# Building a 0/1 matrix from eight columns, moving one batch's sums, and interleaving two projections of v with the first scores

## The chip, the cores and the metric

The kernel runs on one core of a Trainium2 chip. The metric is the device time in microseconds (us). A core has five engines that run side by side and meet at semaphores: PE (TensorE, matrix products; PEld are its weight loads), DVE (VectorE), ACT (ScalarE), POOL (GpSimd) and SP (SyncE, which here only issues DMAs). Each engine works through its own instructions in order. ACT and POOL can issue DMAs too.

## The reference

The reference is two transformer-like layers over x of 4 batches with 512 tokens of 128 values. Only the first layer is touched by the change:

```python
xn = _layernorm(x)
s = _L0_attn_ref(xn, Wq, Wk, Wv, Wo, betas, memory0, z0)
g = _silu(_L0_ffn_ref(xn, Wr, Wg, Wu, Wd, Sg, Su, Sd, expert_bias))
x = x + s * g
```

`_L0_ffn_ref` is a mixture of 8 experts of width 64 with a shared expert: the logits `xn @ Wr` choose two experts for each token, whose probabilities stand in a row `rw` of 8 values (the others are 0); the result is `sum_e rw[e] * (silu(xn @ Wg[e]) * (xn @ Wu[e])) @ Wd[e]` plus the shared expert. `_L0_attn_ref` has 16 heads of width 64 and goes through the sequence in segments of 64 tokens:

```python
scores = q @ k.T * scale            # masked inside the segment
att_dot = softmax(scores) @ v
att_mem = sq @ M / (sq @ Z.T)       # sq = elu(q) + 1, state of all earlier segments
M, Z = M + sk.T @ v, Z + sk.sum()   # sk = elu(k) + 1
out = (gate * att_mem + (1 - gate) * att_dot) @ Wo
```

## The kernel before

The tokens stand as 16 tiles of 128, four to a batch. The program is written out as straight code. Most instructions are pinned (`self.pin`, `mm1`, `act1`, `vec1`): each engine keeps them in the order in which the program names them. Plain GpSimd instructions and DMAs are not pinned, and are placed by a scheduler.

**Loads.** `load_first` issues the 16 tiles of x (12 from SP, 4 from ACT), then from POOL wr, ebias, sg, su and sd, and from SP, behind x, wg, wu, wd and the weights of the attention (lines 120 to 168).

**The first feed-forward stage**, `norm_ffn0`. PE is first warmed with 16 products. `begin0` builds on POOL what the routing needs: `pick0`, a matrix of 96 x 512 zeros and ones in bf16 that spreads the 8 weights of a token over the 64 rows of each expert (line 356 on: a memset, six `affine_select`, each over 32 rows, and a copy to bf16), a bf16 identity, and two zeroed tiles `parts0`. Then batch 0 is brought in: `sums` (line 307: two VectorE instructions, bn_stats and bn_aggr, for each tile), `norm_scale` (root on ACT, reciprocal on DVE), `normed` (line 325: four VectorE instructions that write xn), `turned` (four transposes on PE, one copy to xnT on ACT), `logits`, `shared` (products pg_s and pu_s with sg and su), `chosen` and `weights` (VectorE: the two largest logits of each token, their probabilities in three bf16 parts).

The main loop has 16 steps (b, j), batch by pair of experts. A step makes pg and pu on PE (with wg and wu), h = silu(pg) on ACT, then the preceding step's `down` (products eo with wd, of h that is done by then), pw = pick0 x part on PE, and on DVE h = h * pu (line 559) and h = h * pw (line 560). At the end of a step stands a list `then[(b, j)]` of what prepares later batches. In the kernel before, `sums` of batch 3 stands in the list of step (0, 2), behind `shared_h` and `weights` of batch 1; the list of step (0, 3) has the root over batches 2 and 3 and the normalization of batch 2.

**The first attention**, `attn0`. A half batch h (256 tokens, four segments, each for two independent row groups) is projected by the 12 chunks that `project(h)` returns: 4 of k and 4 of q (`chunk`: products pp, evicted by ACT to pj), 4 of v (`chunk_v`: product pv, evicted to a tile vt, by DVE for h of 0 and 1 and by ACT later, then stored by a DMA from SP to vd in DRAM). `values(n)` loads v of segment n back from vd in another order, as vone (two DMAs from SP). PSUM is shared by `narrow` tiles (two buffers: pp, pv, pk, pa) and `wide` tiles (three buffers: sc, mm, mu, dot, po). vt has two buffers.

The work of a segment n is: `elu_exp` (two ACT instructions) and `elu` (one DVE instruction) for q (0) and k (1); `scores` (products sc, DVE minimum to E); `scores_exp` (ACT); `memory` (products mm, DVE reciprocal and t, POOL times gate); `keys` (transposes pk, ACT copy sk); `update` (products mu, DVE sum to mz); `attend` (products dot, DVE to t, POOL times gate2 and plus t); `attended` (transposes pa). Before the loop over the 32 segments a prologue projects half batch 0, and starts segment 0 and half of segment 1. In the loop, iteration n does the scores of n + 1, memory, update and attend of n, and some chunks of the next half batch's projection: four in iterations 0, 1 and 2, where iteration 0 takes the chunks of v of half batch 1, and 1 and 2 those of k and q.

After these stages follow the second layer's mixture of experts and its attention. They are not changed.

Of the kernel before, what the change touches and what calls it, by code (L numbers as in the profile page):

```python
# [12 lines left out]
F32 = mybir.dt.float32  # L13
# [26 lines left out]
NE, F0 = 8, 64  # L40
# [62 lines left out]
def bc(ap, axis, n):  # L103

    shape = list(ap.shape)
    return ap.unsqueeze(axis).to_broadcast(shape[:axis] + [n] + shape[axis:])


class Kernel:
# [242 lines left out]
    def begin0(self, pool):  # L352


        nc = self.nc
        pick = pool.tile([96, NE // 2, 2, F0], F32, name="pick0")
        nc.gpsimd.memset(pick, 1.0)
        for at in range(0, 96, 32):
            for sign in (1, -1):
                part = pick[at : at + 32]  # L360
                nc.gpsimd.affine_select(
                    out=part, in_=part, pattern=[[-2 * sign, NE // 2], [-sign, 2], [0, F0]],
                    compare_op=ALU.is_ge, fill=0.0, base=0, channel_multiplier=sign,
                )
        self.pick0 = pool.tile([96, NE // 2, 2, F0], BF16, name="pick0b")
        nc.gpsimd.tensor_copy(self.pick0, pick)
        self.identb = pool.tile([P, P], BF16, name="identb")
        nc.gpsimd.tensor_copy(self.identb, self.ident)
        self.parts0 = []
        for k in range(2):  # L370
            t = pool.tile([P, 4, 96], BF16, name=f"parts{k}")
            nc.gpsimd.memset(t, 0.0)
            self.parts0.append(t)

    def norm_ffn0(self, layer, aside=None):
# [4 lines left out]
        nc, tc = self.nc, self.tc  # L380
        v = nc.vector
        xnT, g0 = ([self.of_batch(w, layer, b) for b in range(B)] for w in ("xnT", "g"))
        with tc.tile_pool(name=f"f0_{layer}", bufs=1) as pool, tc.tile_pool(
            name=f"f0p_{layer}", bufs=1, space=PSUM
# [17 lines left out]
            now, xn, lg, rw, part, hs, eo = {}, {}, {}, {}, {}, {}, {}  # L402
# [91 lines left out]
            def down(b, j, h, w):  # L494
# [12 lines left out]
            first = {(b, 0): [(spread, b)] for b in range(B)}  # L507
            then = {
                (0, 0): [(turned, 1), (sums, 2), (more, 1)],
                (0, 1): [(logits, 1), (shared, 1), (chosen, 1)],  # L510
                (0, 2): [(shared_h, 1), (weights, 1), (sums, 3)],
                (0, 3): [(self.norm_scale, mv, rstd, slice(8, 16)), (normed, 2)],
                (1, 0): [(turned, 2), (normed, 3)],
                (1, 1): [(logits, 2), (shared, 2), (chosen, 2)],
# [53 lines left out]
    def attn0(self, xnT, g0, stack, psum, between):  # L568
# [4 lines left out]
        nc, tc = self.nc, self.tc  # L573
# [27 lines left out]
        def project(h):  # L601


            if h >= 2 * B:
                return []
            qkv[h] = dst = [
                pool.tile([P, 32, 64], F32, name=f"pj{h}_{wi}", tag=f"pj{wi}")
                for wi in range(2)
            ]
            vd[h] = drams.tile([2, P * 16, DK], F32, name=f"vd{h}", tag="vd")  # L610
            def chunk_v(p, k):
                ps = narrow(f"pv{h}_{p}_{k}")
                self.mm1(
                    ps, lhsT=xnT[h // 2][:, h % 2 * 2 + p, :],
                    rhs=self.wqkv[2][:, k * S : (k + 1) * S], start=True, stop=True,
                )
                t = pool.tile([P, S], F32, name=f"vt{h}_{p}_{k}", tag="vt")
                if h > 1:
                    self.act1(t, ps, AF.Copy)
                else:  # L620
                    self.vec1(nc.vector.tensor_copy(t, ps))
                nc.sync.dma_start(
                    out=vd[h][p].rearrange("(q k c) d -> k q (c d)", k=2, c=8)[k], in_=t
                )

            def chunk(wi, cq):
                ps = narrow(f"pp{h}_{wi}_{cq}").rearrange("p (c k) -> p c k", c=4)
                for c4 in range(4):
                    c = cq * 4 + c4
                    for p in range(2):  # L630
                        self.mm1(
                            ps[halves[p], c4, :],
                            lhsT=self.wqkv[wi][:, c * 64 : c * 64 + 64],
                            rhs=xnT[h // 2][:, h % 2 * 2 + p, :], start=True, stop=True,
                        )
                view = dst[wi].rearrange("d k (t c) -> d (k t) c", c=16)
                self.act1(
                    view[:, :, cq * 4 : cq * 4 + 4], ps.rearrange("d c k -> d k c"), AF.Copy
                )
            qk = [(lambda wi=wi, cq=cq: chunk(wi, cq)) for wi in (1, 0) for cq in range(4)]  # L640
            v = [(lambda p=p, k=k: chunk_v(p, k)) for p in range(2) for k in range(2)]
            return v + qk if h else qk[:4] + v + qk[4:]
# [5 lines left out]
        def scores(n):  # L648

            q, k = blocks(n, 0), blocks(n, 1)  # L650
            ps = wide(f"sc{n}")
            for hp in range(4):
                for p in range(2):
                    for a in range(2):
                        self.mm1(
                            ps[halves[a], p, hp * 64 : hp * 64 + 64],
                            lhsT=k[halves[p], 2 * hp + a, :], rhs=q[halves[p], 2 * hp + a, :],
                            start=True, stop=True,
                        )
            e = pool.tile([P, 2, 4, LSEG], F32, name=f"E{n}", tag="E")  # L660
            self.vec1(nc.vector.tensor_tensor(  # L661
                e, ps[:, :, 0:256].rearrange("p x (hp c) -> p x hp c", hp=4),
                bc(bc(self.cap, 1, 4), 1, 2), ALU.min,
            ))
            seg[n]["e"] = e

        def scores_exp(n):
            e = seg[n]["e"]
            self.act1(e, e, AF.Exp, scale=1.0 / math.sqrt(DK))
# [4 lines left out]
        def elu_exp(n, w):  # L674
            t = pool.tile([P, 8, 64], F32, name=f"elu{w}{n}", tag=f"elu{w}")
            up = pool.tile([P, 8, 64], F32, name=f"up{w}{n}", tag="up")
            self.act1(t, blocks(n, w), AF.Exp)
            self.act1(up, blocks(n, w), AF.Relu)
            seg[n][w] = t, up

        def elu(n, w):

            t, up = seg[n][w]
            self.vec1(nc.vector.scalar_tensor_tensor(t, t, 1.0, up, ALU.min, ALU.add))  # L684
            seg[n][w] = t
# [11 lines left out]
        def keys(n):  # L697
            t = pool.tile([P, 4, 2, DK], F32, name=f"sk{n}", tag="sk")
            self.act1(t, turn(n, seg[n][1], "pk"), AF.Copy)
            seg[n]["sk"] = t  # L700

        def values(n):

            for p in range(2):
                src = vd[n // 4][p].rearrange("(s hp r) d -> s r hp d", s=4, hp=4)
                nc.sync.dma_start(out=vone[n % 4][:, :, p, 0:DK], in_=src[n % 4])
# [107 lines left out]
        for i, chunk in enumerate(todo):  # L814
            chunk()
            if i == 4:
                elu_exp(0, 1)
            if i == 7:
                elu(0, 1)
            if i == 9:  # L820
                keys(0)
        for n in range(2):
            values(n)
        elu_exp(0, 0)
        scores(0)
        scores_exp(0)
        elu(0, 0)
        elu_exp(1, 1)
        elu(1, 1)
        for n in range(nseg):  # L830
            if n == 0 or n % 4 == 3:
                todo = project((n + 1) // 4 + 1)
            each = 4 if n < 3 or n % 4 != 2 else 0
            nxt = n + 1 < nseg
            more = nxt and not last(n + 1)
            if n + 2 < nseg:
                values(n + 2)
            if nxt:
                elu_exp(n + 1, 0)
                scores(n + 1)  # L840
            memory(n)
            if nxt:
                elu(n + 1, 0)
            if n > 1:
                attended(n - 2)
            if more:
                keys(n + 1)
            if not last(n):
                update(n)
            for f, *args in between.get(n - 0.5, []):  # L850
                f(*args)
            attend(n)
            ahead = n + 2 < nseg and not last(n + 2)
            if ahead:
                elu_exp(n + 2, 1)
            chunks, todo = todo[:each], todo[each:]
            for chunk in chunks[:1]:
                chunk()
            if nxt:
                scores_exp(n + 1)  # L860
            if ahead:
                elu(n + 2, 1)
            for chunk in chunks[1:]:
                chunk()
            for f, *args in between.get(n - 0.25, []):
                f(*args)
            if n % 4 == 2 and n > 4:
                output(n // 4 - 1)
            if not nxt:
                attended(n - 1)  # L870
            for f, *args in between.get(n, []):
                f(*args)
# [1601 lines left out]
```

## Time and profile before

| | us |
|---|---|
| median of 3 runs (from 721.18 to 721.28) | 721.2 |
| the profiled execution | 722.03 |
| its span, first to last instruction | 720.4 |
| PE busy, of the span | 678.1 (94%) |
| DVE busy | 503.7 (70%) |
| ACT busy | 490.9 (68%) |
| POOL busy | 345.7 (48%) |
| first feed-forward stage, up to the first product of the attention | 79.0 |
| attention up to the first product of half batch 1's keys | 107.2 |
| mean granted TensorE clock | 0.991 |

The profile is that of one execution. A row of a timeline or a group reads: start, length, engine, line, operation, what it writes and reads by the names in the program, form, and in brackets the idle time of the engine before it and what ended that. Products, activations and copies that go through helpers all stand at line 336 or 339; the tile's name tells them apart. The granted clock is the share of full speed at which PE was allowed to run. A matrix product of f32 with 512 columns shows as two records.

### The profile page before, as it was taken

How to read it: one execution, taken by the hardware profiler on the slowest of the kernel's cores; microseconds unless marked ns; L12 is line 12 of the kernel's file. 1: busy time of each engine (PE TensorE's matmuls, PEld its weight loads, DVE VectorE, ACT ScalarE, POOL GpSimd, SP SyncE). 2: the span in 40 equal slices, each digit the busy share in tenths (PEclk: the TensorE clock that was granted, in tenths of full speed). 3: DMA queues.
4: the chain of work that ended last, by engine and by line, in shares of the span. 5: the costliest groups of instructions: out<-in, count | busy, mean ns of one | idle time of the engine just before them, and what ended most of it. 6: DMA issues, size and time to landing. Idle time of an engine off the chain costs nothing.

```text
span 720.4 us, 23270 instructions
## 1 busy us (share of the span) xinstructions
PE 678.1 (94%) x9888; PEld 418.1 (58%) x9891; DVE 503.7 (70%) x1078; ACT 490.9 (68%) x809; POOL 345.7 (48%) x381
## 2 busy tenths in 40 slices
PE   7999879999999899979999999999999999999994
PEld 4666557878879677867777783332335233422433
DVE  6776365667576775884549324889896999588854
ACT  3423457877777885653563468989987899899830
POOL 7680027566666574693754423411482844312250
PEclk9999999999999998999999999999999999999999
DMA  7740143231331312100034249967949494955200
GB/s 184 135 134 0 56 129 79 67 106 40 97 106 33 105 30 78 39 12 1 1 98 153 74 146 213 255 168 174 240 148 221 109 250 129 217 143 144 59 17 19
DMA packets 84847, 79.42 MB, mean 110 GB/s; under 512 B 42512, under 2 KB 73520, under 8 KB 81664
## 3 DMA queue, kind: packets, MB, share of 16 engines
q1 hardware_dynamic: 81904, 75.12, 39.6%
q0 software_dynamic: 2256, 2.47, 1.8%
q8 instruction: 80, 1.31, 0.8%
q10 hardware_dynamic: 576, 0.26, 0.1%
q14 instruction: 31, 0.25, 0.1%
HBM read 51.62 MB, written 26.21 MB: 108 GB/s over the span
## 4 chain that ended last, share of the span: by engine, by line
PE 70%; DVE 12%; ACT 10%; issue 4%; DMA 2%; POOL 1%; SPq 0%; DVEq 0%; ACTq 0%; POOLq 0%
PE acc L336 9%; PE pp L336 8%; ACT e L339 7%; PE eo L336 7%; PE po L336 5%; PE ph L336 4%; PE b L336 3%; PE pv L336 3%; PE s L336 3%; PE pl L336 3%; PE sc L336 2%; PE pa L785 2%; PE pg L336 2%; PE pu L336 2%; PE dot L336 2%
## 5 line engine op out<-in xcount | busy, mean ns | idle before, releaser
L339 ACT ACTIVATE e<-s 128x1024 f32<-128x1024 f32 x124 | 121.9, 1056 | 13.8 <-PE s L336 12.7
L336 PE MATMUL acc<-e,strip 128*32 128x512 f32 x1000 | 124.6, 598 | 0.9 <-DVE e L1874 0.9
L339 ACT ACTIVATE e<-e 128x1024 f32<-128x1024 f32 x104 | 107.4, 1094 | 0.0
L736 POOL TENSOR_TENSOR t<-t,gate 128x512 f32<-128x512 f32 x32 | 49.7, 1554 | 66.0 <-DVE t L717 66.0
L336 PEld LDWEIGHTS acc<-e,strip 128*32 128x32 f32 x1000 | 28.6, 109 | 70.4 <-issue 59.2
L774 POOL TENSOR_TENSOR t<-t,gate 128x512 f32<-128x512 f32 x32 | 50.7, 1585 | 31.0 <-DVE sums L773 24.6
L339 ACT ACTIVATE pj<-pp 128x512 f32<-128x512 f32 x64 | 38.5, 602 | 21.2 <-PE pp L336 21.0
L684 DVE SCALAR_TENSOR_TENSOR elu<-elu,up 128x512 f32<-128x512 f32 x60 | 48.0, 801 | 5.3 <-ACT up L339 5.3
L661 DVE TENSOR_TENSOR E<-sc,cap 128x512 f32<-128x512 f32 x32 | 22.0, 688 | 40.2 <-PE sc L336 40.2
L339 ACT ACTIVATE h<-ph 128x1024 f32<-128x1024 f32 x20 | 20.5, 1023 | 38.3 <-PE ph L336 31.0
L339 ACT ACTIVATE attT<-pa 128x128 f32<-128x128 f32 x128 | 25.0, 284 | 28.5 <-PE pa L785 28.1
L336 PE MATMUL s<-q,k 64*128 64x512 bf16 x256 | 40.9, 382 | 3.5 <-ACT e L339 3.3
L336 PEld LDWEIGHTS <-k 64*128 64x128 bf16 x256 | 8.8, 94 | 59.6 <-issue 58.6
L775 POOL TENSOR_TENSOR t<-t,t 128x512 f32<-128x512 f32 x32 | 41.8, 1307 | 2.5
L336 PE MATMUL eo<-w_out,h 128*128 128x128 f32 x320 | 39.6, 278 | 0.0
L336 PEld LDWEIGHTS eo<-w_out,h 128*128 128x128 f32 x320 | 37.6, 192 | 3.4 <-issue 1.9
L339 ACT ACTIVATE elu<-pj 128x512 f32<-128x512 f32 x60 | 38.5, 642 | 0.1
L1714 POOL TENSOR_TENSOR pr<-pr,pr 128x512 f32<-128x512 f32 x14 | 22.5, 1629 | 33.4 <-DVE pr L1709 33.3
L339 ACT ACTIVATE up<-pj 128x512 f32<-128x512 f32 x60 | 38.4, 639 | 0.0
L336 PE MATMUL pp<-xnT,l0Wq 128*64 128x128 f32 x512 | 31.2, 277 | 3.2 <-ACT attT L339 2.2
L1623 DVE TENSOR_TENSOR second<-second,first 128x1024 f32<-128x1024 f32 x16 | 27.0, 1694 | 9.0 <-DMA second<-qf 9.0
L1157 POOL TENSOR_SCALAR th<-th 128x512 f32<-128x512 f32 x4 | 2.5, 617 | 64.2 <-ACT th L339 64.2
(331 smaller groups left out, 1641.9 us busy)
## 6 DMA issues: line engine op xcount, KB each, us to landing
vd<-vt SPq DMA_DIRECT2D x32, 256.0 KB
vone<-vd SPq DMA_DIRECT2D x64, 128.0 KB
first<-qe SPq DMA_DIRECT2D x8, 1024.0 KB
second<-qf SPq DMA_DIRECT2D x16, 512.0 KB
third<-qf SPq DMA_DIRECT2D x32, 256.0 KB
qf<-qT SPq DMA_DIRECT2D x64, 64.0 KB
k<-kd SPq DMA_DIRECT2D x16, 256.0 KB
q<-qd SPq DMA_DIRECT2D x16, 256.0 KB
```

The costliest lines, as they stand in the source:

```text
L336: return self.pin(self.nc.tensor.matmul(*args, **kw))
L339: return self.pin(self.nc.scalar.activation(*args, **kw))
L661: self.vec1(nc.vector.tensor_tensor(e, ps[:, :, 0:256].rearrange("p x (hp c) -> p x hp c", hp=4), bc(bc(self.cap, 1, 4), 1, 2), ALU.min,))
L684: self.vec1(nc.vector.scalar_tensor_tensor(t, t, 1.0, up, ALU.min, ALU.add))
L736: nc.gpsimd.tensor_mul(t, t, self.gate)
L774: nc.gpsimd.tensor_mul(t, t, gate2)
L775: nc.gpsimd.tensor_add(t, t, seg[n]["t1"])
L785: self.pin(nc.tensor.transpose(ps[:, hp, :], seg[n]["att"][:, hp].rearrange("i p v -> i (p v)"), self.ident,))
L1157: self.pool1(self.nc.gpsimd.tensor_scalar(t, t, 0.5, 0.5, ALU.mult, ALU.add))
L1623: self.vec1(self.nc.vector.tensor_mul(t, t, self.first1[mm][:, two]))
L1714: self.nc.gpsimd.tensor_add(self.prod1[b, m], self.prod1[b, m], t)
```

## The change

```diff
@@ begin0
-        pick = pool.tile([96, NE // 2, 2, F0], F32, name="pick0")
+        pick = pool.tile([96, NE // 2, 2], F32, name="pick0")
         nc.gpsimd.memset(pick, 1.0)
...
-                    out=part, in_=part, pattern=[[-2 * sign, NE // 2], [-sign, 2], [0, F0]],
+                    out=part, in_=part, pattern=[[-2 * sign, NE // 2], [-sign, 2]],
...
-        nc.gpsimd.tensor_copy(self.pick0, pick)
+        nc.gpsimd.tensor_copy(self.pick0, bc(pick, 3, F0))
@@ norm_ffn0
-                (0, 1): [(logits, 1), (shared, 1), (chosen, 1)],
-                (0, 2): [(shared_h, 1), (weights, 1), (sums, 3)],
+                (0, 1): [(logits, 1), (shared, 1), (chosen, 1), (sums, 3)],
+                (0, 2): [(shared_h, 1), (weights, 1)],
@@ attn0
+        ahead = project(1)
         for n in range(2):
             values(n)
+        ahead.pop(0)()
         elu_exp(0, 0)
+        elu(0, 0)
         scores(0)
-        scores_exp(0)
-        elu(0, 0)
         elu_exp(1, 1)
         elu(1, 1)
+        ahead.pop(0)()
+        scores_exp(0)
         for n in range(nseg):
-            if n == 0 or n % 4 == 3:
+            if n % 4 == 3:
                 todo = project((n + 1) // 4 + 1)
-            each = 4 if n < 3 or n % 4 != 2 else 0
+            elif n == 0:
+                todo = ahead
+            each = 2 if n == 0 else 4 if n < 3 or n % 4 != 2 else 0
```

The 0/1 matrix is made as 96 x 8 values; the copy to bf16 repeats each of them 64 times (`bc` is a view with a step of 0). The sums of batch 3 are named one step sooner, behind `chosen` of batch 1, which puts them before the two multiplications of h of step (0, 2) instead of before those of step (0, 3).

In the attention, the first chunk of v of half batch 1 goes before the first scores, and the second between `scores` of segments 0 and 1; the other two remain in iteration 0. In the engines' orders this gives: PE pv, sc (segment 0), pv, sc (segment 1), mm, pk, mu, dot, pv, pv; DVE vt, elu of q of segment 0, E of segment 0, elu of k of segment 1, vt, E of segment 1. `scores_exp(0)` stands behind `elu_exp(1, 1)` on ACT. On SP, the store of the first chunk comes before the last of the loads of segment 3's v, and the second right after that load. Number and shapes of products, activations and DMAs are as before.

## The prediction

> **What bounds the kernel now.** I read the chain of waits over the first 125 us, then each engine's timeline there, then busy time by stretches. The page's summary of the chain says what kind of kernel this is: TensorE (PE) carries most of it, so a microsecond of PE idle time that ends on another engine is a microsecond of the end, unless a later wait takes it back.
>
> ```profile
> PE 70%; DVE 12%; ACT 10%; issue 4%; DMA 2%; POOL 1%; SPq 0%; DVEq 0%; ACTq 0%; POOLq 0%
> ```
>
> The change touches three places, and the chain (start, length, what) leaves PE in all of them:
>
> ```profile
> 6.15 2.88 DVE xn L325 x4
> ...
> 11.37 1.91 PE pg_s L336 x2
> ...
> 32.65 2.05 PE eo L336 x16
> ```
>
> VectorE's timeline (the bracket is the idle time before) shows the first: four normalizations take 2.87 us, and the same four take 1.11 us ten microseconds later.
>
> ```profile
> 6.15 2.87 DVE L325 TENSOR_SCALAR xn<-x,mv,rstd 128x128 f32<-128x128 f32 x4
> ...
> 16.04 1.11 DVE L325 TENSOR_SCALAR xn<-x,mv,rstd 128x128 f32<-128x128 f32 x4
> ...
> 25.47 0.69 DVE L559 TENSOR_TENSOR h<-h,pu 128x512 f32<-128x512 f32 x1 [1.45 <-PE pu L336]
> ```
>
> GpSimd's timeline shows what ran beside the slow four: the wide selects of the 0/1 matrix, each next to one normalization, one every 0.72 us on both engines. The second line is a select of few columns, 0.2 us each.
>
> ```profile
> 5.35 3.59 POOL L361 TENSOR_SCALAR_AFFINE_SELECT pick<-pick 32x512 f32<-32x512 f32 x5
> ...
> 39.08 0.59 POOL L1193 TENSOR_SCALAR_AFFINE_SELECT of<-of 128x4 f32<-128x4 f32 x3
> ```
>
> Busy time by stretch (PE, PEld, DVE, ACT, POOL, then the granted clock) shows that the thin first stretch is followed by 3.4 us at half the clock:
>
> ```profile
> 7.39:10.80 3.41, 1.69 (x10) 1.12 (x10) 3.09 (x11) 0.75 (x2) 3.06 (x7) 1.00 0.43 114
> 10.80:14.21 3.41, 3.41 (x8) 1.86 (x8) 2.63 (x20) 2.43 (x5) 3.37 (x6) 0.50 1.14 272
> 270.21:273.63 3.42, 2.56 (x12) 1.26 (x10) 0.35 (x2) 1.52 (x3) 2.67 (x2) 1.00 0.56 203
> ```
>
> And PE's timeline at the start of the attention shows holes in front of nearly every step, ended by VectorE:
>
> ```profile
> 95.05 1.00 PE L336 MATMUL mm<-mz,elu 64*64 64x65 f32 x32 [0.95 <-DVE elu L684]
> 96.97 0.63 PE L691 MATMUL pk<-ident,elu 128*128 128x128 f32 x4 [0.92 <-DVE elu L684]
> ...
> 101.24 1.12 PE L336 MATMUL pv<-l0Wv,xnT 128*128 128x512 f32 x2 [0.64 <-DVE vt L621]
> 103.05 1.12 PE L336 MATMUL pv<-l0Wv,xnT 128*128 128x512 f32 x2 [0.69 <-DVE vt L621]
> ```
>
> **Part 1, the 0/1 matrix.** GpSimd: the memset (0.54) becomes some 0.15 by the smallest memsets of its timeline; six selects of 0.67 become six of 0.2 by the row above; the copy to bf16 still writes 96x512 and keeps its 0.61. Nothing waits for the matrix itself: it was ready at 11.3 and is first read at 17.4. So by itself this is worth nothing; the 3.2 us that GpSimd gains are hidden, and its later loads merely start sooner. What counts is the normalization beside it, which is on the chain.
> How much faster does it get? A memset, the last selects and a copy still run on GpSimd from 6 to 7.7. The Trainium skill (SBUF — State Buffer, "Who interferes with whom") says that a VectorE operation in a two-port mode and a GpSimd operation exclude each other for the whole instruction. By that rule alone each of the four still waits out one short operation: 4 x (0.28 + 0.2) = 1.9, a gain of 1.0. The nearest row is the normalization at 35.56, which took 1.11 with two GpSimd copies of 128x128 inside it: a gain of 1.76. Against it stands a VectorE cast of 0.70 instead of 0.17 at 40.74, amid 42 tiny memsets. I take the row, 1.76, and keep 1.0 as the other end.
> What is late next: PE at present reaches pg_s at 11.2 and runs it, pu_s and half of pg at half clock (1.91 against 0.96 at 21.83). With 1.76 less, pg_s starts at 9.4, and the stretch 7.39 to 10.80 has more work. Counting each record's columns at 0.43 us per 512, that stretch held 11% array work and 270.21 to 273.63 held 37%; both were followed by half clock. The least that was not is 43%, at 75.7. With pg_s from 9.4 it is about 45%, so the drop should go. Then PE would reach pg at 11.0; but pg needs wg and pu needs wu, whose transfers land at 12.5 and 13.6 by the trace's landing events (packets under 512 bytes, which are these two, run until 12.9). So the loads bind: pu starts at 13.6 instead of 15.5. GpSimd's load l1bqf, now issued near 7.9 instead of 11.25, puts one packet of 4 KB and 0.16 us on each DMA engine, before or amid wg: 13.8. Gain **1.7**. The parts of the router weights (VectorE, ready at 15.4 - 1.8 = 13.6) do not bind pu, and wd lands at 17.4, ahead of its first use near 18. With the low end, 1.0, the drop stays, and pu_s and pg run at half speed: gain 1.3.
>
> **Part 2, sums of batch 3.** Four pairs of statistics, 29.53 to 31.13, are 1.60 us ahead of the two multiplications for h of step (0,3); PE waits for these until 32.65. They move to 23.9, where VectorE sits idle 1.45 us until pu (row above): they end at 25.5 and delay the multiplication at 25.47 by 0.1, and the one after it waits for pw until 26.51 anyway. The x tiles have been in since 10.6. Then h is ready at 31.0 and PE, free after the transposes of part 1's weights at 31.08, goes on without its 1.41 us hole. Next would be ScalarE: its two table loads around the root (27.98 and 31.57, 1.28 each) run one after the other once the sums are early, so the next Silu is at 30.9 instead of 32.87, and part of batch 1 near 31.4, before PE wants it at 32.9. The normalization of batch 2 begins at 31.2 instead of 32.7. Gain 32.65 - 31.08 = **1.55**.
>
> **Part 3, projections of v.** No work is added; two of the four chunks (PE 0.95, VectorE copy 0.69, one DMA from SP each) move ahead. I replay the engines in the old times, from 92.27, where PE ends pp and used to wait 0.7 for ScalarE. pv 0 runs there to 93.2, sc 0 to 93.7 (0.3 later than before), pv 1 to 94.65, sc 1 to 95.2. VectorE: copy of pv 0 to 93.95, elu(0,0) to 94.8, E 0 to 95.4, elu(1,1) to 96.0 (was 96.8, since ScalarE now makes its inputs before the exponential of E 0), copy of pv 1 to 96.6, E 1 to 97.2. PE: mm at 95.2, pk at 96.1 (was 96.97), mu 96.6, dot at 97.25 when E 1 has freed its PSUM buffer (was 98.04). The remaining two chunks follow to 99.6 without the DMA waits at 103.3 and 105.1, because only two are left for two buffers. VectorE then goes through the first segment (rm, t, elu, mz, rd, t, sums) to 100.4, one copy to 101.05, elu(2,1) to 102.25 (it took 1.29 beside GpSimd's multiplication before, and stands beside it again), the last copy to 102.9, E 2 to 103.5. PE: pk at 102.3, dot at 103.55, the pp chunks at 104.05. They were at 107.18: gain **3.1**.
> Bounds: if the copies' 2 x 0.69 ahead of elu and E are paid in full because VectorE is the bound from 93 to 103, it is 1.7; 3.6 if elu(2,1) is not held up. On SP, the store of pv 0 now stands ahead of the last of segment 3's v loads; that load is wanted after 113, so the wait costs nothing. The other loads queue behind stores that come earlier than before. On ScalarE the exponential of E 0 is behind two more activations (1.04 us), but E 0 itself is ready only at 95.4, as they end.
>
> **Sum.** 1.7 + 1.55 + 3.1 = 6.35. The profiled execution took 722.03 (span 720.4), 0.8 over the median of 721.2: its span would be 714.0, itself 715.7, and the median **714.9**. Behind 107 us the same instructions follow in the same order, all earlier, with no load from the start still pending.
>
> **Rivals.**
> - The clock moves elsewhere (0.3). The half-speed stretches begin on a grid of 3.41 us. If the grid keeps still, the thin part at 270 to 275 falls 6.35 earlier on it. Its half speed (273.6 to 280.5) costs about 2.5 us: sc to dot take 4.7 instead of some 2.6, lp 0.5 to 0.8 more. If it vanishes: 712.4. If another thin place takes a new one, such as the new hole at 100.5 to 102.3 or the stretch at 249 (about 30% on some grids), one window costs up to 1.7: 716.6. The Trainium skill (TensorE: Matmul & The Clock Gate, "What's actually happening") asks for an idle window before the drop; by it neither new hole of 1.8 us would drop the clock. The row of 270.21, with 2.56 us busy, did, so I don't rely on the rule.
> - Part 3 gives only its low end, VectorE the bound (0.15): 714.9 + 1.4 = 716.3.
> - Part 1 does nothing, because the short GpSimd operations still hold VectorE or wg and wu come later (0.07): 716.6.
> - Slower (0.04): the thin places left by waiting for wg and by VectorE in the attention, and the shifted grid at 249 and 308, each cost a window at half speed: 1.7 apiece, so from the fourth additional one it is over: 714.9 + 4 x 1.7 = 721.7. Against it: before has only two such places in 720 us.
>
> **How the numbers follow.** The forecast as worked out has 0.44: 714.9, by itself 713.8 to 716. Range 712.0 to 718.3: both clock cases and two low ends together. A difference under 0.2% (1.4 us) can't be told from none. Faster by more takes in everything up to 719.8: 0.91. Within: 0.05. Slower: 0.04.
>
> **What would show it.** xn at 6.15 takes about 1.1 us; no half clock at 10.8; pg waits for wg's landing and pu for wu's; no hole before eo near 29.4 and the Silu after it earlier by 3; pp of the second half at 100.8 or so (107.18 - 6.35) and no wait for a store in front of vt. Wrong if xn stays over 2 us, if the hole before eo only turns into one ended by ScalarE, or if pk in the second segment waits until its old place.

## The result and the profile after

| | before | after |
|---|---|---|
| median, us (6 runs each) | 721.24 (721.18 to 722.51) | 716.47 (713.16 to 717.44) |
| ratio, 95% interval | | 0.992 (0.9897 to 0.9944) |
| the profiled execution, its span | 722.03, 720.4 | 716.71, 715.3 |
| first transposes of batch 1 | 17.61 | 17.45 |
| from there to the first product of the attention | 61.38 | 59.76 |
| from there to the first product of half batch 1's keys | 28.19 | 25.16 |

The change is faster, by 0.8%. Forecast were 714.9 and a range of 712.0 to 718.3: the time lies in the range, 1.6 above the forecast. The last three rows of the table divide the gain by the three parts: the second and third gave what was forecast (1.62 and 3.03 us), and the first gave 0.16 instead of 1.7. So the number held because the range left room for such a miss, not because every part was right.

The page's summary of the chain, beside that of before, has two points of VectorE less and one of DMA more:

```profile
PE 70%; DVE 10%; ACT 10%; issue 4%; DMA 3%; SPq 1%; POOL 1%; DVEq 0%; ACTq 0%; POOLq 0%
```

Why, VectorE's and GpSimd's timelines show first (start, length, engine, line, operation, tiles, and in brackets the idle time before and what ended it). GpSimd in the changed kernel:

```profile
4.93 0.72 POOL L361 TENSOR_SCALAR_AFFINE_SELECT pick<-pick 32x8 f32<-32x8 f32 x3
...
8.18 0.57 POOL L240 DMA_DIRECT2D l1bqf<-in_L_attn_bq_dram  x1
```

VectorE in the changed kernel:

```profile
6.10 1.12 DVE L325 TENSOR_SCALAR xn<-x,mv,rstd 128x128 f32<-128x128 f32 x4
...
25.39 0.67 DVE L559 TENSOR_TENSOR h<-h,pu 128x512 f32<-128x512 f32 x1
...
99.11 1.30 DVE L684 SCALAR_TENSOR_TENSOR elu<-elu,up 128x512 f32<-128x512 f32 x1
```

PE in the changed kernel:

```profile
10.52 1.02 PE L336 MATMUL pu_s<-xnT,su 128*128 128x512 f32 x2
13.79 1.13 PE L336 MATMUL pg<-xnT,wg 128*128 128x512 f32 x2 [2.25 <-DMA wg<-in_L_ffn_Wg_dram]
15.10 1.12 PE L336 MATMUL pu<-xnT,wu 128*128 128x512 f32 x2 [0.18 <-DMA wu<-in_L_ffn_Wu_dram]
...
17.45 0.60 PE L419 MATMUL lnt<-ident,xn 128*128 128x128 f32 x4
...
30.70 0.39 PE L488 MATMUL rwt<-identb,parts 128*96 128x128 bf16 x4
30.92 1.11 PE L336 MATMUL eo<-wd,h 128*128 128x128 f32 x8
...
100.46 0.66 PE L691 MATMUL pk<-ident,elu 128*128 128x128 f32 x4 [1.19 <-DVE elu L684]
...
102.37 3.89 PE L336 MATMUL pp<-xnT,l0Wk 128*64 128x128 f32 x64
```

The reader is to see: xn fell from 2.87 to 1.12, and pu_s runs at 10.5 at full clock. Then PE stands still for 2.25 us, because wg, which landed at 12.48 in before, lands at 13.74, and wu at 15.05 instead of 13.59. The chain of waits now holds one long DMA in this place (start, length, what):

```profile
9.57 5.48 DMA wu<-in_L_ffn_Wu_dram
15.10 1.12 PE pu L336 x2
```

The hole of 1.41 in front of eo is gone (30.92 follows rwt at once), and the keys of half batch 1 start 25.2 after the attention's first product.

What made two loads of SP later, which the change doesn't touch? GpSimd's load l1bqf, issued at 8.18 instead of 11.25, now falls amid wg. The DMA view from 9 to 11 us of the changed kernel shows the two kinds of queue (packets, MB, share of the 16 engines' time in the stretch); q0 is GpSimd's, q1 is that of SP and ACT:

```profile
q0 software_dynamic: 33, 0.07, 41.8%
q1 hardware_dynamic: 294, 0.12, 21.7%
```

The same stretch of before:

```profile
q1 hardware_dynamic: 898, 0.29, 58.6%
```

33 packets of GpSimd hold the engines for 41.8% of 2 us, and q1 gets a third of its packets through. l1bqf is 16 of the 33, one of 4 KB on each engine; by the trace's packet records they took 0.22 to 1.57 us each, where most packets of 4 KB of sg and su had taken 0.16. The other 17 packets have 4 or 32 bytes. That l1bqf is the culprit, and why, was left to experiments.

### The profile page after: what moved, and what is told of

The parts are those of the page before. It is cut to its first block, busy times and chain, and to the rows that moved or that the text cites. A ratio compares the mean times of both kernels' runs of the same rounds, so it can differ in the third digit from the quotient of the medians.

```text
span 715.3 us, 23273 instructions
## 1 busy us (share of the span) xinstructions
PE 676.8 (95%) x9891; PEld 417.3 (58%) x9891; DVE 501.3 (70%) x1078; ACT 491.1 (69%) x809; POOL 344.4 (48%) x381
## 4 chain that ended last, share of the span: by engine, by line
PE 70%; DVE 10%; ACT 10%; issue 4%; DMA 3%; SPq 1%; POOL 1%; DVEq 0%; ACTq 0%; POOLq 0%
PE acc L336 9%; PE pp L336 8%; PE eo L336 7%; ACT e L339 7%; PE po L336 5%; PE ph L336 4%; PE pl L336 3%; PE s L336 3%; PE b L336 3%; PE pv L336 2%; PE pa L785 2%; PE pu L336 2%; PE sc L336 2%; PE pg L336 2%; PE dot L336 2%
## 5 line engine op out<-in xcount | busy, mean ns | idle before, releaser
L339 ACT ACTIVATE e<-s 128x1024 f32<-128x1024 f32 x124 | 121.9, 1054 | 13.8 <-PE s L336 13.1
L336 PE MATMUL pp<-xnT,l0Wk 128*64 128x128 f32 x512 | 32.0, 277 | 0.9 <-ACT g L339 0.7
```

Source lines behind the costliest of these rows:

```text
L336: return self.pin(self.nc.tensor.matmul(*args, **kw))
L339: return self.pin(self.nc.scalar.activation(*args, **kw))
```

## The experiments

Theory L: part 1 gains nothing because GpSimd's earlier bias loads delay wg and wu; without that it gains its time. The rivals: part 1 gains nothing for another reason (the clock, VectorE, GpSimd), or the late landing is an accident of one execution. The level of before differs between the five groups of runs (721.2, 721.0, 716.9, 720.6 and 715.1 us), so that each ratio is taken within a group. And the runs of one kernel spread by some us, so that the timelines carry the verdicts on parts of a microsecond. All starts of the table are from the profiled execution of the kernel.

| kernel | ratio to before (95%) | wg, wu land | transposes of batch 1 | to the attention | to the keys |
|---|---|---|---|---|---|
| before | 1 | 12.48, 13.59 | 17.61 | 61.38 | 28.19 |
| e1_matrix | 0.9994 (0.9973 to 1.0016) | 13.29, 14.60 | 17.00 | 61.29 | 28.17 |
| e2_sums | 0.9967 (0.9953 to 0.9981) | | 16.90 | 60.07 | 28.19 |
| e3_v | 0.9929 (0.9902 to 0.9956) | 12.61, 13.75 | 16.46 | 61.62 | 25.14 |
| after | 0.992 (0.9897 to 0.9944) | 13.74, 15.05 | 17.45 | 59.76 | 25.16 |
| e9_changed (after again) | 0.9949 (0.9929 to 0.9968) | 13.43, 14.53 | 16.93 | 59.76 | 25.13 |
| e4_later | 0.9904 (0.9878 to 0.993) | 12.39, 13.51 | 15.90 | 59.76 | 25.14 |
| e11_later_again | 0.9887 (0.9861 to 0.9913) | 12.46, 13.55 | 15.95 | 60.40 | 25.14 |
| e7_matrix_later | 0.999 (0.9978 to 1.0003) | 12.44, 13.57 | 15.96 | 61.59 | 28.18 |
| e8_small_first | 0.9928 (0.99 to 0.9955) | 12.54, 13.82 | 16.22 | 59.78 | 25.14 |
| e5_early | 0.9924 (0.9903 to 0.9944) | no wait | 15.77 | 59.76 | 25.15 |
| e6_both | 0.9918 (0.9901 to 0.9935) | no wait | 15.37 | 59.77 | 25.15 |
| e10_warm | 0.9889 (0.9864 to 0.9914) | no wait | 16.82 | 59.76 | 25.14 |

### The parts alone

e1_matrix, e2_sums and e3_v are before with the part of the diff under begin0, under norm_ffn0 and under attn0 alone; nothing else differs.

> The kernel before with the narrow 0/1 matrix alone. Theory L (GpSimd's loads of the second layer's biases, issued 3 us sooner, stand in front of wg and wu on the DMA engines): the four normalizations take about 1.1 us instead of 2.87 and PE is done with pu_s near 11.4, but wu lands near 15.0 instead of 13.6, so the transposes of batch 1 start at 17.4 to 17.5, against 17.61 before: median 720.9 to 721.3. Theory C (the loads land as before, the changed kernel lost time to half-clock stretches that fall elsewhere): wu lands near 13.6, the transposes of batch 1 start near 16.0, median 719.5.

> The kernel before with the sums of batch 3 a step sooner, alone. The prediction's step 2: no idle time of PE in front of eo after the transposes of the router weights of batch 1, eo at 31.1 instead of 32.65, median 719.7. Rival (the hole only turns into one ended by ScalarE's table loads): eo of batch 1 or pw waits for part, gain under 0.5, median above 720.7.

> The kernel before with two projections of v ahead, alone. The prediction's step 3: first product pp of half batch 1's keys at 104.1 instead of 107.2, median 718.1. Rival (VectorE is the bound, the copies ahead of elu and E are paid): 105.5 and 719.5.

Measured: 0.9994, 0.9967 and 0.9929, that is 0.4, 2.4 and 5.1 us of 721, each with an uncertainty of 1 to 2 us. The table's columns are sharper: only the kernels with part 2 have 60.4 or less to the attention where it was 61.3 to 61.6 (most of them 59.76, 1.7 us less), and only those with part 3 have 25.1 instead of 28.2 to the keys (3.04 us), to a tenth in every profile. The 5.1 of e3_v (3.2 to 7.1) is more than these 3.04; why was not found. The matrix alone makes xn short (1.29) and gains no time that can be measured. wu lands at 14.60 and batch 1 starts at 17.00: late, as by theory L, though less so than its 15.0 and 17.4. Its PE shows the same wait as in after:

```profile
13.34 1.12 PE L336 MATMUL pg<-xnT,wg 128*128 128x512 f32 x2 [1.82 <-DMA wg<-in_L_ffn_Wg_dram]
14.65 1.13 PE L336 MATMUL pu<-xnT,wu 128*128 128x512 f32 x2 [0.18 <-DMA wu<-in_L_ffn_Wu_dram]
```

Something else came from the two kernels without the matrix edit: their batch 1 starts at 16.90 and 16.46, not at 17.61. In both, VectorE waited less for the x tiles: xn begins at 5.74 and 5.71, not at 6.15, and ends at 8.31, not at 9.02. That is 0.71 us, all that e2_sums has. VectorE in e2_sums:

```profile
5.74 2.57 DVE L325 TENSOR_SCALAR xn<-x,mv,rstd 128x128 f32<-128x128 f32 x4
```

The other 0.44 of e3_v goes with the clock. Its start has no half clock, although its matrix is as wide as before (xn 2.60). Its stretches (start to end, length, busy time of PE, PEld, DVE, ACT and POOL, the granted clock, and the DMAs' share and GB/s):

```profile
8.95:12.37 3.42, 2.88 (x12) 1.57 (x12) 2.78 (x21) 2.06 (x4) 3.18 (x6) 1.00 0.80 187
```

And those of e2_sums, on another grid, with half clock as in before:

```profile
7.70:11.11 3.41, 2.34 (x12) 1.60 (x13) 2.80 (x15) 1.76 (x3) 3.11 (x6) 1.00 0.49 126
11.11:14.53 3.42, 3.42 (x5) 1.28 (x4) 2.91 (x22) 2.60 (x5) 3.06 (x6) 0.50 1.18 298
```

So the 17.61 of the profile that the prediction was made from is one draw; the three draws without the edit have a mean of 17.0.

### The loads kept back

e4_later is the changed kernel in which GpSimd's bias loads wait for wu: a copy of one column of wu into the tile that the load fills stands ahead of it.

```diff
             flat = aside.tile([P, D], F32, name=f"l1b{w}f")
+            if w == "q":
+                nc.gpsimd.tensor_copy(flat[:, 0:1], self.wu[:, 0, 0:1])
             nc.gpsimd.dma_start(out=flat, in_=i[f"L1_attn_b{w}"].partition_broadcast(P))
...
                 self.b1[w] = pool.tile([P, 1], F32, name=f"l1b{w}")
+                nc.gpsimd.tensor_copy(self.b1[w], self.wu[:, 0, 0:1])
```

> The changed kernel, where GpSimd copies one column of wu into the bias tiles before it loads them, so that those loads start only when wu has landed. Theory L: wg lands near 12.5 and wu near 13.6, as in the kernel before; pu of step (0,0) starts at 13.6 to 13.7 instead of 15.10, the transposes of batch 1 start 1.4 sooner than in the changed kernel, median 1.4 below its 716.5: 715.1. Theory C: no difference beyond the spread of the changed kernel, median 716 to 717.

PE of e4_later:

```profile
12.44 1.12 PE L339 MATMUL pg<-xnT,wg 128*128 128x512 f32 x2 [1.57 <-DMA wg<-in_L_ffn_Wg_dram]
13.55 1.13 PE L339 MATMUL pu<-xnT,wu 128*128 128x512 f32 x2
...
15.90 0.60 PE L422 MATMUL lnt<-ident,xn 128*128 128x128 f32 x4
```

wg and wu land where they landed in before, and batch 1 starts at 15.90, 1.55 earlier than in after. Ratio 0.9904; the median, 715.01, is what was expected. Theory L holds by the timeline; the ratio alone would not show it, since its interval overlaps that of the changed kernel. The same again, beside the later runs:

> e4_later once more, beside the other two: wu at 13.6, transposes of batch 1 at 15.9 (16.3 where the warming ends late), ratio to before 0.990 to 0.993; by theory L 0.2% below the changed kernel, whose two ratios were 0.992 and 0.995.

0.9887 (its interval ends at 0.9913, below that of e9_changed) and 15.95. On the way to the attention this one lost 0.64: a VectorE cast to bf16 near 27.4 took 0.78 instead of 0.18, with GpSimd issuing two loads beside it. Holding GpSimd's work back moves it beside other work; the collision wasn't tried by itself.

e7_matrix_later is before with the matrix edit and this same wait:

> The kernel before with the matrix edit alone, where GpSimd's bias loads wait for wu. With these loads not waiting, the matrix edit alone was worth 0.999 (0.997 to 1.002). Theory L: the edit is worth its time once the loads stay behind wu; wg lands near 12.4, wu near 13.5, transposes of batch 1 at 15.9 against 17.0 in e1_matrix and 16.5 to 17.6 in three profiles without the edit: 1.1 below before, ratio 0.9985. Rival: half clock or another wait takes it, ratio 1.000 and transposes at 16.5 or later.

Batch 1 starts at 15.96 against 17.00 in e1_matrix: the edit has its 1.0 us against the mean of the draws once the loads stay behind. The interval of the ratio, 0.9978 to 1.0003, holds both the forecast and none: it can't tell them apart.

The changed kernel again tells whether the late landing was an accident:

> The changed kernel once more, as the common measure for these three: 716.5, with wu landing near 15 and the transposes of batch 1 near 17.4. If those late loads were an accident of the one profiled execution (the rival to theory L), wg and wu land here near 12.5 and 13.6 and the transposes of batch 1 start near 15.9.

wu lands at 14.53 and batch 1 starts at 16.93: late again, by 1.0 instead of 1.5. In all eight kernels with the matrix edit whose wg and wu stand behind x (e12_plain, below, is one), batch 1 starts 2.4 us behind wu's landing, from 13.51 and 15.90 (e4_later) to 15.05 and 17.45 (after): wu's landing decides the start.

### Which load, and why it is slow

e8_small_first lets the four small loads l1bq go early, and only l1bqf and what is behind it waits for wu:

```diff
+            if w == "q":
+                self.b1[w] = pool.tile([P, 1], F32, name=f"l1b{w}")
+                ownq = i[f"L1_attn_b{w}"].rearrange("(r m d o) -> m r d o", m=4, r=4, o=1)
+                for m in range(4):
+                    self.pool1(nc.gpsimd.dma_start(out=self.b1[w][m * 32 : m * 32 + 32], in_=ownq[m]))
+                self.pool1(nc.gpsimd.tensor_copy(flat[:, 0:1], self.wu[:, 0, 0:1]))
```

> The changed kernel, where only the repeated load l1bqf (and all behind it) waits for wu, while the four small loads of l1bq go out early, near 8.2 to 10.5. If the repeated load with its 16 packets of 4 KB is what delays wg and wu: wg lands near 12.4 and wu near 13.5, transposes of batch 1 at 15.9, median 715.0. If it is the small loads (32 packets of 4 bytes each) or the issuing itself: wu near 15, transposes at 17.4, median 716.5.

The DMA view of e8_small_first, 9 to 11 us:

```profile
q1 hardware_dynamic: 806, 0.26, 59.7%
q0 software_dynamic: 64, 0.00, 2.3%
```

64 small packets hold the engines for 2.3%; wg lands at 12.54, wu at 13.82, 0.3 behind e4_later. So the small loads cost some 0.3, and the rest, 0.7 to 1.2, is l1bqf. It reads the same 512 bytes for all 128 partitions. e12_plain tells a load of this size from a load of this kind:

```diff
-            nc.gpsimd.dma_start(out=flat, in_=i[f"L1_attn_b{w}"].partition_broadcast(P))
+            nc.gpsimd.dma_start(
+                out=flat,
+                in_=i["L0_ffn_Sg"] if w == "q" else i[f"L1_attn_b{w}"].partition_broadcast(P),
+            )
```

> The changed kernel, where the load l1bqf at 8.2 us reads the 64 KB of sg (128 rows that lie one behind the other) instead of 128 times the same 512 bytes of the bias; so the second layer's bias of q is replaced by other data. Theory R (the repeated source makes the packets slow): the 16 packets of 4 KB take about 0.2 us each as those of sg did, wg lands near 12.5 and wu near 13.7, transposes of batch 1 at 15.9 to 16.2. Rival (any load of 64 KB that GpSimd brings in there): packets of 1 us and more, wg near 13.5, wu near 14.6 to 15, transposes at 16.9 to 17.5.

With this other bias, the flag that the second attention returns sends the program on into its general version, which computes everything again: 14,779 us. Only the start, before the data differ, is read. The same stretch of e12_plain:

```profile
q1 hardware_dynamic: 682, 0.23, 50.4%
q0 software_dynamic: 70, 0.07, 12.4%
```

The 16 packets, issued at the same time and of the same size, took 0.16 to 0.46 us, most of them 0.16 to 0.2, against 0.22 to 1.57 in after. wg lands at 12.78, wu at 14.01, batch 1 starts at 16.40: a little behind what theory R expected, half a microsecond ahead of e9_changed. So wu's delay of 1.0 to 1.5 us against e4_later falls to 0.5. Of that, 0.3 was there with the small loads alone, which leaves some 0.2 for a plain load in this place, and 0.5 to 1.0 for the repeated source. This rests on one profile. Nor is such a load slow everywhere: l1bkf, of the same kind, took 0.26 to 0.42 us a packet between 20.8 and 24.4 in before, e2_sums and e3_v. What in the traffic of 9 to 18 us makes the difference was not tested.

### wg and wu first

e5_early issues wg and wu on SP right behind the first four x tiles of its queue; e6_both has the wait of e4_later as well.

```diff
+            if n == 7:
+                self.wg = pool.tile([P, NE, F0], F32, name="wg")
+                self.dma1(self.wg, i["L0_ffn_Wg"].rearrange("e d f -> d e f"))
+                self.wu = pool.tile([P, NE, F0], F32, name="wu")
+                self.dma1(self.wu, i["L0_ffn_Wu"].rearrange("e d f -> d e f"))
```

> The changed kernel, with the loads of wg and wu issued on SP right behind the first four x tiles of its queue, ahead of the eight tiles of batches 2 and 3. If the start is bound by wg and wu alone (theory L: they land late because the bias loads of GpSimd fall amid them), they now land before 11 us, ahead of those bias loads, PE goes from pu_s (10.5) straight to pg near 11.5 and pu near 12.6, and the first transposes of batch 1 start at about 15.0 instead of 17.45, where VectorE (hs ready at 13.8, xn at 14.8) binds: median 716.5 - 2.4 = 714.1. The rival, that the last engine to be ready is another one anyway (VectorE behind the x tiles of batches 2 and 3, which now come 2 us later, or wd): transposes at 16 to 17.5, median 715 to 716.5.

> e5_early, and in addition GpSimd's bias loads wait for wu. If the bias loads hurt only through wg and wu, the wait adds nothing to e5_early: transposes of batch 1 at about 15.0, median 714.1, within 0.5 of e5_early. If they also hurt the x tiles or wd, this is the faster one by more than 0.5.

PE of e5_early:

```profile
1.30 6.26 PE L339 MATMUL warmp<-warm 128*128 128x512 bf16 x16 [1.30 <-DVE sums L580]
7.41 0.60 PE L422 MATMUL lnt<-ident,xn 128*128 128x128 f32 x4
...
12.26 1.02 PE L339 MATMUL pu<-xnT,wu 128*128 128x512 f32 x2
14.00 0.40 PE L491 MATMUL rwt<-identb,parts 128*96 128x128 bf16 x4 [0.71 <-DVE parts L484]
...
15.77 0.60 PE L422 MATMUL lnt<-ident,xn 128*128 128x128 f32 x4
```

pg and pu run behind pu_s without a wait, as expected; the transposes come at 15.77 instead of 15.0. VectorE's parts bind, and they come late because all of batch 0 does: its transposes stand behind the 16 products that warm PE, which go on until about 7.5. In before these ended at 6.2, under an xn that went on to 9.0. They run at half clock until the first boundary of the grid, and that lay at 6.67 here, at 3.97 in before. e6_both, with the boundary at 5.86, has 15.37; the two medians, 711.46 and 711.12, are within 0.5 as expected and can't be told apart, and both intervals overlap that of e9_changed (712.92). e10_warm is e6_both with 10 products instead of 16:

```diff
-            for _ in range(16):
+            for _ in range(10):
```

> e6_both with 10 instead of 16 products in PE's warming ahead of the first transposes. In e9_changed the 16 end at 7.9 where xn is done by 6.8, since they run at half clock until 7.33; in before they ended at 6.2, under an xn that went on to 9.0. Theory W: with xn short and wg early the warming is what the first transposes wait for. With 10 it ends by 5.7 whatever the clock, the transposes of batch 0 start near 6.4, pg_s at 8.9 instead of 9.2 (9.9 on the latest grid) and the transposes of batch 1 at 14.8 instead of 15.4: median 0.3 to 0.8 below e6_both's level, ratio 0.991. Rival: fewer products leave PE idle before the grid's next boundary, and the half clock goes on or comes back in 6.5 to 10: pg_s at 10 or later, transposes of batch 1 at 16 or more, ratio 0.993 or more.

PE of e10_warm, then its stretches:

```profile
1.31 3.66 PE L342 MATMUL warmp<-warm 128*128 128x512 bf16 x10 [1.31 <-DVE sums L583]
6.36 0.84 PE L425 MATMUL lnt<-ident,xn 128*128 128x128 f32 x4 [1.39 <-DVE xn L331]
...
9.61 2.05 PE L342 MATMUL pg_s<-xnT,sg 128*128 128x512 f32 x2
```

```profile
4.02:7.44 3.42, 1.78 (x9) 0.67 (x6) 2.85 (x14) 1.21 (x3) 2.98 (x13) 1.00 0.98 231
7.44:10.85 3.41, 2.97 (x10) 2.45 (x11) 2.03 (x14) 1.97 (x3) 2.23 (x6) 0.50 0.70 153
10.85:14.26 3.41, 3.41 (x5) 1.34 (x5) 2.92 (x18) 2.18 (x4) 2.58 (x7) 0.50 0.76 138
```

Both sides of the expectation show in one profile: the transposes start at 6.36, but the window with the hole of 1.39 ahead of them is followed by 6.8 us at half clock, pg_s runs at 9.61 and batch 1 starts at 16.82. The median is nevertheless that of e11_later_again, 713.36 beside 712.82. Whether 10 products are better on other grids stays open. No version was shown to be faster than e4_later.

## Why the prediction was right or wrong

**The step that failed** is the price of one load in part 1: "GpSimd's load l1bqf ... puts one packet of 4 KB and 0.16 us on each DMA engine, before or amid wg: 13.8". The time at which it would be issued was right (near 7.9; it was 8.18), and so was its place amid wg. But its packets took up to 1.57 us, and pu started at 15.10. The 0.16 was that of sg and su, plain loads, and in e12_plain most packets took 0.16 to 0.2 when such a load stood in the place of l1bqf. The trace of before had the right number: its own l1bqf packets, at 14.2 to 15.8, took 0.86 to 2.45 us in all but two cases (0.16). This is the rival with a chance of 0.07, "Part 1 does nothing, because ... wg and wu come later", at 716.6; the median was 716.47. Its mechanism is shown by e4_later and e8_small_first. The other half of that rival, short GpSimd operations that hold VectorE, hardly came: xn took 1.11 or 1.12 in nine profiles with the edit, with selects and a memset beside it, and 1.29 and 1.32 in e1_matrix and e5_early, where one of the four took 0.52 to 0.54 instead of 0.34, beside the memset. So the row of 35.56 was right. The low end had the exclusive lock of the Trainium skill (SBUF — State Buffer, "Who interferes with whom") cost VectorE a wait at each of the four; the runs show one such wait at most, and in after it is a select of GpSimd that took 0.30 instead of 0.20.

**The base of part 1** was wrong too, and would have shown had the loads stayed away. The 1.7 was taken from a start at 17.61 with half clock from 10.8, and that is one draw. What differs between the three draws is first the x tiles, which let xn end at 9.02 or at 8.31 (0.71 us), and then the clock (0.44 us). For the clock, "If the grid keeps still" was the wrong question: the Trainium skill (TensorE: Matmul & The Clock Gate, "What's actually happening") says that the window of about 3.4 us runs freely and does not begin anew with a kernel. The profiles agree: the first boundary lay at 3.97, 6.56, 4.29, 5.54, 4.21, 6.62 and 7.33 in seven of them. With the loads kept back, batch 1 starts at 15.90 to 15.96 in e4_later, e7_matrix_later and e11_later_again, on three grids (4.21, 4.84 and 6.50). So part 1 is worth 1.05 on average (17.0 to 15.95), and 1.7 only against the late draw of before's profile. Two readings were off as well. The 15.5 for pu is the chain's; PE's timeline has 15.36. And the window at 75.7 is not the least that kept its clock: in before 365.78 to 369.19 held 39 to 41% of array work. That the half clock at 10.8 goes came true nevertheless.

**Part 2** (1.55 forecast): 1.62 in the result; against the mean of the four kernels without it (61.47) it is 1.7 by the 59.76 of most kernels that have it, 1.4 by e2_sums and 1.1 by e11_later_again. The sums run at 23.8 to 25.4, the multiplication for h starts at 25.39, ScalarE's two table loads run one after the other and the Silu is at 30.73, as forecast for 30.9.

**Part 3** (3.1): 3.03 to 3.05 in every kernel that has it. The second pk waits for elu(2,1), which took 1.30 beside GpSimd's multiplication, the row that the replay had kept at 1.29. The low end of 1.7 and its rival are out. The forecast place, 100.8, is met by e4_later (100.80); in after it is 102.37, and the difference is that of part 1.

**The clock rival** (0.3): the thin part near 270 kept its half speed (269.4 to 276.3 in after, as long as in before). Which of the thin places at 245, 270 and 308 lose clock changes from profile to profile with the grid, among kernels that are the same there. It moves single runs, and no sign of an effect of the change was seen; of before there is one profile only. **The slower rival** needed four new windows; none came in after.

**The sum**: by the mean of the draws, part 1 is 17.0 less 17.1 (the mean of 17.00, 17.45 and 16.93), that is -0.1, part 2 is 1.6, part 3 is 3.04: 4.5 us or 0.994, against 0.992 and 0.995 measured. With the loads kept back it is 1.05 + 1.6 + 3.04 = 5.7, or 0.992; measured 0.9904 and 0.9887. The first interval holds it; the second ends at 0.9913, 0.6 us short of it. The rest can't be placed: the stretch behind the keys, which no edit touches, took 608.3 to 613.2 us in the thirteen profiles of the table.

## What to carry to other kernels

An engine that becomes free earlier issues its later DMAs earlier: price each of them with the packet times of that same load in the trace, not with those of another load of the same size. A load that repeats one row for all partitions held its DMA engines several times as long as a plain one at the same place; where its packets are slow in the trace, it belongs behind whatever is waited for next. And where a stretch at half clock is part of the base, look at more than one execution before its disappearance is booked as a gain.

## What the runs showed that was not expected

- Packets of 4 KB that repeat 512 bytes: 0.22 to 1.57 us in after, against 0.16 to 0.46 for as many bytes that lie one behind the other, at the same time and place (e12_plain). With 16 such packets and the small loads behind them, two loads of another queue landed 0.9 to 1.5 us later.
- The drop to half clock followed how much of a window the array worked, and no idle window was needed: in before, 270.21 to 273.63 had PE busy for 2.56 of 3.42 us, and half clock came behind it. The count takes 0.43 us for each record of 512 f32 columns at full clock (the distance of the two records of pg), half as much for bf16, and the share of the array's rows and columns that the record uses. In nine profiles (before, after, e1 to e4, e8, e9 and e10) each of the 21 drops ahead of the last microseconds came behind a window of the grid with at most 39% of such work. Windows that were not followed by a drop had 34% or more, so the edge lies at 34 to 39% and this count doesn't make it sharp. In after, 10.03 to 13.44, with the wait for wg, held 37% and kept its clock; in e10_warm it was 32% of 4.02 to 7.44 that was followed by the drop.
- The warming of PE has two prices. With 16 products it ended at 6.2 to 7.9, by where the grid's first boundary lies, and once xn is short it is what the first transposes wait for; with 10 it left, in the one profile, a window thin enough to lose the clock.
